# A state-space stage on one core: another order of the side work, and states multiplied in place

## The chip, the cores and the metric

The kernel runs on one core of a Trainium2 chip. The metric is the device time of one execution in microseconds (us), the median of several runs. The engines are named as in the profile: PE is TensorE, DVE is VectorE, ACT is ScalarE, POOL is GpSimd, and SP is the engine whose queue issues most transfers.

## The reference

The input is an image batch x of shape 4 x 96 x 64 x 64. The first of three blocks turns it into four sequences of 4096 positions with 96 channels and runs two state-space layers over them. A layer is, cut to what matters:

```
h     = layernorm(seq)
xs, z = split(h @ in_w)                       # 192 channels each
xc    = silu(causal_conv4(xs) + conv_b)
dt, B, C = split(xc @ xproj_w)                # 6, 16 and 16 columns
delta = softplus(dt @ dt_w + dt_b)
dA    = exp(delta * A)                        # per channel and 16 states
dBx   = delta * B * xc
state[t] = dA[t] * state[t-1] + dBx[t]        # along the 4096 positions
y     = sum_over_states(state * C) + Dp * xc
seq   = seq + (y * silu(z)) @ out_w
```

A fusion with a pooled vector and a batch norm close the block. A convolution block and an attention and feed-forward block in the frequency domain follow; the change doesn't touch them.

## The kernel before

The function `_mamba` holds the state-space stage. The positions are cut into 8 chunks (ch) of 512, the four sequences into two pairs (pr), and there are two layers (l): 32 *units*. The order of units goes by chunk: layer 0 of pair 0, layer 1 of pair 1 of the chunk before, layer 0 of pair 1, layer 1 of pair 0. A unit has 2 x 192 channels x 16 states. They are done in 24 *steps*: k is the channel block (0 to 2), r the group of rows (0 to 3), h the half (0 or 1), so 768 steps in all. Two steps (h = 0 and 1) make a group g, and share one states tile.

A step s of the main loop does the following, and each engine gets its instructions in just this order, written out by hand:

- `broadcasts` (PE, L447) spreads rows of u = delta * xc over the partitions into a PSUM tile pq. u comes as two parts, ux and uy, so that PE's products keep float32's digits. `product` (DVE, L457) multiplies pq by B in place.
- `decays` (ACT, L452) makes dA from delta, which `copies` (SP, L434) fetches, replicated, from DRAM (ddl) into the tile a five steps ahead.
- In four steps of a unit, numbers 2, 6, 10 and 14 (`apart`; called split steps below), the roles differ: u is fetched replicated into db (from ddu), the product with B is POOL's (L457 with db), and the decay goes to pq.
- `scans` (DVE, L470) runs two scans of 512 positions into the states tile hs, starting from hst, the end states of the chunk before. Between the two scans DVE does the product of the next step, except ahead of a split step. Then POOL multiplies the states by C into a tile hc (L476). hs and hc are rings of two.
- `states` (ACT, L480), after every second step, copies the last column of hs to hst.
- `reduce` (PE, L488) sums over the states, three steps after a group began. `gate` (DVE L496, POOL L497) makes y of a channel block after eight steps.

Beside this runs *side work*, in generators that yield between pieces; `Side.slot` emits one piece, and the loop gives one slot to each step (two in the units numbered 0, 1 and 30). There are these lanes. `front(unit)` makes the inputs of the next unit: projections mm_i (L264, L267), silu (L279, L280), mm_dbl (L287, L290) with dbl, dh and dx (L293 to L303), mm_d (L311, L313) with dl (L315), the transfers bc, softplus (L322, emitted in L601), ddl, du = delta * xc on POOL (L339), and the parts ux, uy and ul (L352, L355) with their transfers. `tail(unit)` is the output projection mm_o (L369 to L371) of the unit before, from step 3 on; its result is s (L375), or ft in the second layer (L380). `norm(unit)` is the layer norm of the unit after next, from step 10 on: mm_xc (L203), xc and sq on ACT (L197, L199), mm_v (L214), ve, vh and r on ACT, twelve small Newton steps for the inverse root on POOL (L227 to L230), mm_r (L240), and hn on DVE (L249). `rest` holds batch statistics. At the end of a unit `side.drain()` emits all side work that is left.

Of the kernel before, what the change touches and what calls it, by code (L numbers as in the profile page):

```python
# [48 lines left out]
def _mamba(ctx, tc, io, w, fd, fstats, xsums):  # L49
# [26 lines left out]
    A, HS, HC = ("a", 0, 2, 6), ("hs", 0, 4, 2), ("hc", 0, 4, 2)  # L76
# [12 lines left out]
    out_wT = staged(io["out_wT"], "out_wT", [C, 2, 128], *HC)  # L89
# [12 lines left out]
    dtH = stage("dtH", [128, NL, 256], *HC)  # L102
# [66 lines left out]
    seq, made, ys = {}, {}, {}  # L169
    pqs, das, dbs, hss, hcs, pys = {}, {}, {}, {}, {}, {}  # L170
# [18 lines left out]
    def norm(unit):  # L189

        ch, l, pr = unit
        bs = (2 * pr, 2 * pr + 1)
        xc, sqs, ps = {}, {}, {}

        def centred(n):
            xc[n] = tl(f"xc{n}", unit, [C, TC])
            nc.scalar.copy(xc[n], ps[n])  # L197
            sqs[n] = tl(f"sq{n}", unit, [C, TC])
            nc.scalar.activation(sqs[n], xc[n], AF.Square)  # L199

        for n, b in enumerate(bs):
            ps[n] = mm(f"xc{n}", unit, [C, TC])
            nc.tensor.matmul(ps[n], ctr, seq[b, ch, l], start=True, stop=True)  # L203
            if l == 0:
                nc.scalar.activation(
                    tl("xs", unit, [C, TC], to=f"sq{n}"), seq[b, ch, 0], AF.Identity, accum_out=xsums[:, b, ch : ch + 1]
                )
            yield
            centred(n)
            yield "free" if n == 0 else "gap"  # L210
        p_v = mm("v", unit, [128, 8])
        for n in range(2):
            for j in range(4):
                nc.tensor.matmul(  # L214
                    p_v[:, n * 4 + j : n * 4 + j + 1], sqs[n][:, j * 128 : (j + 1) * 128], mean1, start=True, stop=True
                )
        yield
        ve = tl("ve", unit, [128, 8])
        r = tl("r", unit, [128, 8])
        vh = tl("vh", unit, [128, 8])  # L220
        a = tl("ra", unit, [128, 8])
        nc.scalar.activation(ve, p_v, AF.Identity, bias=w["eps"])
        nc.scalar.activation(vh, ve, AF.Copy, scale=-0.5)
        yield "gap"
        nc.scalar.activation(r.bitcast(I32), ve.bitcast(I32), AF.Identity, bias=magic, scale=-0.5)
        for _ in range(3):
            nc.gpsimd.tensor_tensor(a, r, r, ALU.mult)  # L227
            nc.gpsimd.tensor_tensor(a, a, vh, ALU.mult)
            nc.gpsimd.tensor_scalar(a, a, 1.5, None, ALU.add)
            nc.gpsimd.tensor_tensor(r, r, a, ALU.mult)  # L230
        if ch:
            for b in bs:
                hn = hn_buf[b, l]
                nc.scalar.copy(hn[:, 0:3], hn[:, TC:])
        yield "gap"
        yield "gap"
        for n, b in enumerate(bs):
            p = mm(f"r{n}", unit, [C, TC])
            for j in range(4):
                nc.tensor.matmul(  # L240
                    p[:, j * 128 : (j + 1) * 128],
                    r[:, n * 4 + j : n * 4 + j + 1].to_broadcast([128, C]),
                    ident,
                    start=True,
                    stop=True,
                )
            yield
            yield
            nc.vector.tensor_tensor(hn_buf[b, l][:C, 3:], p, xc[n], ALU.mult)  # L249
            yield "free"  # L250

    def front(unit):

        ch, l, pr = unit
        bs = (2 * pr, 2 * pr + 1)
        for j in range(6):
# [13 lines left out]
            if j == 0:  # L270
                xcv = tl("xcv", unit, [128, 3, TC], bufs=2)
            if j == 3:
                zs = tl("zs", unit, [128, 3, TC], bufs=2)
# [29 lines left out]
        nc.gpsimd.tensor_tensor(dx, dbl, lo, ALU.add)  # L303
        yield "gap"
        dl = tl("dl", unit, [128, 3, TC])
        bcs = []
        for k in range(3):
# [8 lines left out]
            if k == 1:  # L316
                for at in range(2):
                    t = tl(f"bc{at}", unit, [128, 2, TC], bufs=2)
                    src = ddb[at].rearrange("s n t -> s (n t)")[:, None].to_broadcast([DS, 8, 2 * TC])
                    nc.sync.dma_start(t.rearrange("p n t -> p (n t)"), src)  # L320
                    bcs.append(t)
# [6 lines left out]
        us, parts, dus, cut = [], [], [], []  # L328
        made[unit] = [xcv, zs, *bcs, dd, us, parts]
        for at in range(6):  # L330
# [26 lines left out]
            yield "gap"  # L357

    def tail(unit):
# [4 lines left out]
        for n in range(2):  # L364
# [13 lines left out]
            else:  # L378
                ft = work.tile([C, TC], F32, name=f"ft_{tag(unit)}_{n}", tag="ft", bufs=2)
# [6 lines left out]
    def way_out(unit):  # L386
# [11 lines left out]
        for n in range(2):  # L398
            b = 2 * pr + n
            nc.vector.bn_stats(fstats[:, b, ch, :], po[:C, n, :])  # L400
            ft = work.tile([C, TC], F32, name=f"ft_{tag(unit)}_{n}", tag="ft", bufs=2)
# [57 lines left out]
    def scans(s):  # L459
# [15 lines left out]
        sl = slice(2 * h, 2 * h + 2)  # L475
        (nc.gpsimd if s + 1 < n_steps else nc.vector).tensor_tensor(hcs[g][:, sl, :], hss[g][:, sl, :], bc(unit, 3, k, h), ALU.mult)  # L476

    def states(g):
        ch, l, pr = steps[2 * g][0]
        nc.scalar.copy(hst[pr, l, g % 12], hss[g][:, :, TC - 1])  # L480

    def reduce(g):
# [3 lines left out]
        hc = hcs.pop(g)  # L486
# [13 lines left out]
    class Side:  # L500
# [26 lines left out]

        def drain(self):
# [4 lines left out]
    n_steps = len(steps)  # L533
    with tc.manual_schedule():
# [3 lines left out]
        side.drain()  # L538
        for s in range(5):
# [7 lines left out]
        for s in range(n_steps + NS):  # L547
# [33 lines left out]
            if n == 0 or n + 1 in late:  # L581
# [5 lines left out]
            if live and s + 5 < n_steps:  # L587
                unit, k, r, h = steps[s + 5]
                while unit not in made or apart(s + 5) and len(made[unit][5]) <= k:
                    side.slot()  # L590
                copies(s + 5)
# [4 lines left out]
            if at == NS - 1 and n + 1 < len(units):  # L596
                side.drain()
# [956 lines left out]
```

## Time and profile before

| what | value |
|---|---|
| median of 3 runs | 5238.29 us (5235.17 to 5256.56) |
| profiled execution | 5239.08 us |
| its span in the profile | 5237.3 us |
| the state-space stage in it | 93 to 3085 us |
| share of the span busy: PE, DVE, ACT, POOL | 78%, 83%, 51%, 57% |
| mean granted clock of PE | 0.819 |

A row of a waits view gives the engine and instruction that waited, what was taken to release it, the total in us, how often, and the longest. In a timeline a row gives start, duration, engine, line, operation, output and inputs with their shapes, and in brackets the idle time before it with its supposed releaser. The releaser is inferred from semaphore events; where an instruction waits for several, the one named need not be the one that was late. A row of a lines view ends with busy time, mean duration in ns, and the idle time before.

### The profile page before, as it was taken

To read this page: it belongs to the slowest core of one execution; us is meant where nothing else is said; L and a number is where in the kernel's file an instruction comes from. 1 tells how busy PE (TensorE), PEld (TensorE's weight loads), DVE (VectorE), ACT (ScalarE), POOL (GpSimd) and SP (SyncE) were. 2 spreads that over 40 slices of the span, in tenths; PEclk is the share of its full clock that TensorE was granted. 3 is DMA by queue.
4 is the path that set the end of the run, shared out by engine and by line. 5 is a ranking of instruction groups with operands and counts; after the bars stand their busy time and mean duration, and the time that the engine had idled before them with its cause. 6 is when DMAs were issued, how large, how long until landed. Compare 5 with 4: busy or idle time off the path is not lost.

```text
span 5237.3 us, 52687 instructions
## 1 busy us (share of the span) xinstructions
PE 4069.8 (78%) x15440; PEld 1747.5 (33%) x15440; DVE 4322.3 (83%) x5639; ACT 2693.7 (51%) x5149; POOL 2988.1 (57%) x2105
## 2 busy tenths in 40 slices
PE   5677777777777777777777637899898899989776
PEld 2222222222222222222222102345455555545565
DVE  2879899898989989899998887879787978787655
ACT  3565666656566665656656520024453544434566
POOL 2878888888888888888888860002130312212122
PEclk7767877777787777778787658999999999999977
DMA  4768888888887888888788765553325233332110
GB/s 100 179 168 192 197 193 205 195 197 195 197 195 192 209 196 193 195 197 202 186 208 196 175 168 157 165 174 94 95 86 155 85 98 97 100 90 79 53 33 21
DMA packets 314046, 800.19 MB, mean 153 GB/s; under 512 B 52247, under 2 KB 58106, under 8 KB 312702
## 3 DMA queue, kind: packets, MB, share of 16 engines
q1 hardware_dynamic: 310174, 790.53, 59.8%
q10 hardware_dynamic: 3584, 6.29, 0.4%
q8 instruction: 123, 2.02, 0.2%
q14 instruction: 165, 1.35, 0.1%
HBM read 703.83 MB, written 67.63 MB: 147 GB/s over the span
## 4 chain that ended last, share of the span: by engine, by line
PE 26%; DVE 24%; issue 15%; POOL 11%; ACT 9%; DMA 7%; SPq 1%; DVEq 0%; POOLq 0%; ACTq 0%
DVE hs L470 10%; PE py L895 10%; DVE pq L457 6%; DMA a<-ddl 5%; POOL hc L476 4%; PE py L488 2%; DVE z L880 2%; ACT a L452 2%; DVE a L1110 2%; PE px L1177 2%; PE ph L1092 2%; PE pa L1078 2%; PE mm_i L264 2%; POOL t L1248 1%; PE pv L1133 1%
## 5 line engine op out<-in xcount | busy, mean ns | idle before, releaser
L476 POOL TENSOR_TENSOR hc<-hs,bc 128x1024 f32<-128x1024 f32 x767 | 1803.2, 2360 | 318.4 <-DVE hs L470 305.7
L470 DVE TENSOR_TENSOR_SCAN hs<-a,hst,pq 128x512 f32<-128x512 f32 x1280 | 1575.0, 1263 | 40.1 <-ACT hst L480 17.3
L895 PE MATMUL py<-z,wk 128*96 128x512 f32 x2304 | 1113.1, 612 | 25.0 <-issue 14.0
L452 ACT ACTIVATE a<-a,aneg 128x512 f32<-128x512 f32 x1280 | 846.1, 711 | 223.4 <-DMA a<-ddl 216.1
L880 DVE TENSOR_TENSOR z<-cp,cp 128x512 f32<-128x512 f32 x1152 | 794.9, 717 | 183.7 <-PE py L895 169.0
L457 DVE TENSOR_TENSOR pq<-pq,bc 128x1024 f32<-128x1024 f32 x640 | 773.2, 1208 | 111.6 <-PE pq L447 111.5
L488 PE MATMUL py<-hc,red 128*32 128x512 f32 x3072 | 672.3, 840 | 39.4 <-POOL hc L476 39.4
L895 PEld LDWEIGHTS py<-z,wk 128*96 128x96 f32 x2304 | 366.9, 169 | 448.7 <-issue 318.9
L447 PE MATMUL pq<-uy,sel 64*128 64x512 f32 x768 | 262.9, 643 | 281.1 <-DVE hs L470 275.1
L470 DVE TENSOR_TENSOR_SCAN hs<-pq,hst,db 128x512 f32<-128x512 f32 x256 | 325.5, 1271 | 148.1 <-POOL dx L303 95.0
L1145 POOL MEMSET zz<- 96x2 f32 x16 | 1.6, 98 | 738.5 <-ACT zz L1154 738.5
L264 PE MATMUL mm_i<-hn,wk 97*128 97x512 f32 x512 | 297.7, 710 | 118.3 <-ACT xcv L275 93.2
L1246 POOL TENSOR_TENSOR o<-o,fb 128x384 f16<-128x384 f16 x64 | 67.0, 1047 | 547.1 <-ACT o L1251 544.1
L452 ACT ACTIVATE pq<-a,aneg 128x512 f32<-128x512 f32 x256 | 177.0, 692 | 343.5 <-DMA a<-ddl 249.3
L457 POOL TENSOR_TENSOR db<-db,bc 128x1024 f32<-128x1024 f32 x128 | 302.0, 2360 | 23.8 <-DMA db<-ddu 23.8
L447 PEld LDWEIGHTS pq<-uy,sel 64*128 64x128 f32 x768 | 97.9, 234 | 568.4 <-DVE hs L470 431.7
L447 PE MATMUL pq<-ux,sel 64*128 64x512 f32 x512 | 181.5, 635 | 96.4 <-DVE hs L470 76.6
L275 ACT ACTIVATE xcv<-mm_i,pvec 128x512 f32<-128x512 f32 x96 | 66.0, 687 | 313.1 <-PE mm_i L264 147.8
L1177 PE MATMUL px<-bd,a 128*96 128x128 f32 x1024 | 148.2, 293 | 67.1 <-DVE a L1110 56.2
L1146 POOL TENSOR_TENSOR zz<-zz 96x256 f32<-96x256 f32 x128 | 122.8, 959 | 133.4 <-ACT zz L1153 81.3
L264 PEld LDWEIGHTS mm_i<-hn,wk 97*128 97x128 f32 x512 | 98.7, 214 | 291.1 <-issue 165.5
L447 PEld LDWEIGHTS pq<-ux,sel 64*128 64x128 f32 x512 | 66.9, 231 | 305.3 <-DVE hs L470 212.0
(286 smaller groups left out, 6534.3 us busy)
## 6 DMA issues: line engine op xcount, KB each, us to landing
a<-ddl SPq DMA_DIRECT2D x768, 512.0 KB, 6.8
cp<-p SPq DMA_DIRECT2D x480, 192.0 KB, 2.7
db<-ddu SPq DMA_DIRECT2D x128, 512.0 KB, 9.0
bc<-ddb SPq DMA_DIRECT2D x64, 512.0 KB, 7.8
cp<-p SPq DMA_DIRECT2D x480, 64.0 KB, 2.7
ddl<-dl SPq DMA_DIRECT2D x128, 192.0 KB, 3.9
tw_k_fwd<-in_k_fwd SPq DMA_DIRECT2D x64, 256.0 KB, 3.4
tw_k_inv<-in_k_inv SPq DMA_DIRECT2D x64, 256.0 KB, 3.1
```

Source lines behind the costliest of these rows:

```text
L264: nc.tensor.matmul(p, wt[:, 0:128], hn_buf[bs[k], l][:, cols], **f)
L447: nc.tensor.matmul(pqs[s][:, i, :], sel[rows, r, :], made[unit][6][k][h][rows], start=True, stop=True)
L452: nc.scalar.activation(to[:, i, :], das[s][:, i, :], AF.Exp, scale=acol(s, i))
L457: engine.tensor_tensor(t, t, bc(unit, 2, k, h), ALU.mult)
L470: nc.vector.tensor_tensor_scan(hss[g][:, at, :], d0[:, i, :], d1[:, i, :], hst[pr, l, g % 12][:, at : at + 1], ALU.mult, ALU.add)
L476: (nc.gpsimd if s + 1 < n_steps else nc.vector).tensor_tensor(hcs[g][:, sl, :], hss[g][:, sl, :], bc(unit, 3, k, h), ALU.mult)
L488: nc.tensor.matmul(pys[unit, k][32 * (i // 2 + i % 2 * 2) :][:32], red[:, r, :], hc[:, i, :], start=(r == 0), stop=(r == 3))
L880: nc.vector.tensor_tensor(zs[n], cps[q, r0], cps[q, r1], ALU.mult)
L895: nc.tensor.matmul(pys[q], wk[k // KG][:, k % KG, :], zs.pop(n), start=(k == 0), stop=(k == NE - 1))
L1078: nc.tensor.matmul(pa[j][:, jj, :], kf[:, 2 * (j % 2) + jj, :], dd[j][:, jj, :], start=True, stop=True)
L1146: nc.gpsimd.tensor_tensor(z0[:, :, 0, :], z0[:, :, 0, :], z1[:, :, 0, :], ALU.add)
L1177: nc.tensor.matmul(p[:, j, :], a2[i % 2][:, kk, :], tabs["bd"][:, int(kk > 0), :], start=True, stop=True)
```

## The change

What it does, in the order of the diff:

- The side work has another order. `front` of a unit may begin a whole unit earlier: at step 4 of unit n, norm and front of unit n+2 are queued together (the latter in a lane of its own, `ahead`, that becomes the front lane at the next unit's start), and front waits until its norm is done. The loop gives a second slot in every odd step, so 36 a unit for 24, and the drain at a unit's end is gone.
- `front` ends with du; the fetches bc and ddu and the parts ux, uy and ul move into a generator `split`, in a lane that comes first, and are made one channel block at a time (steps 5, 13 and 21 of the unit before its own).
- dx on POOL is not issued where it is made but kept in `side.post` and issued behind the next product with C.
- Copies may stay behind and catch up (`copied`), where they had to be five steps ahead.
- States are multiplied by C in place, in hs, without the last column; hs becomes a ring of three and hc is gone. ACT multiplies the last column, after the copy to hst, with one or two small instructions per group.
- xcv and zs are rings of three, and ft uses the buffers of sq.

```diff
             nc.vector.tensor_tensor(hn_buf[b, l][:C, 3:], p, xc[n], ALU.mult)
+            if n == 1:
+                normed.add(unit)
             yield "free"
 
     def front(unit):
 
         ch, l, pr = unit
         bs = (2 * pr, 2 * pr + 1)
+        while unit not in normed:
+            yield "gap"
...
-                xcv = tl("xcv", unit, [128, 3, TC], bufs=2)
+                xcv = tl("xcv", unit, [128, 3, TC], bufs=3)
...
-                zs = tl("zs", unit, [128, 3, TC], bufs=2)
+                zs = tl("zs", unit, [128, 3, TC], bufs=3)
...
         dx = tl("dx", unit, [128, TC], F32R)
-        nc.gpsimd.tensor_tensor(dx, dbl, lo, ALU.add)
+        side.post.append(lambda: nc.gpsimd.tensor_tensor(dx, dbl, lo, ALU.add))
         yield "gap"
         dl = tl("dl", unit, [128, 3, TC])
-        bcs = []
         for k in range(3):
...
-            if k == 1:
-                for at in range(2):
-                    t = tl(f"bc{at}", unit, [128, 2, TC], bufs=2)
-                    src = ddb[at].rearrange("s n t -> s (n t)")[:, None].to_broadcast([DS, 8, 2 * TC])
-                    nc.sync.dma_start(t.rearrange("p n t -> p (n t)"), src)
-                    bcs.append(t)
         _softplus(nc, work, dl)
         yield "gap"
 
         dd = dp.tile([2, 32, 3, 2, TC], F32, name=f"ddl_{tag(unit)}", tag="ddl")
         for q in range(4):
             nc.sync.dma_start(dd[q % 2, :, :, q // 2, :], dl[32 * q : 32 * q + 32])
-        us, parts, dus, cut = [], [], [], []
-        made[unit] = [xcv, zs, *bcs, dd, us, parts]
-        for at in range(6):
+        us, parts, dus = [], [], []
+        made[unit] = [xcv, zs, None, None, dd, us, parts]
+        while side.low:
+            yield "gap"
+        for ks in ((0, 1), (2,)):
+            for k in ks:
+                dus.append(tl(f"du{k}", unit, [128, TC], to="du", bufs=3))
+                nc.gpsimd.tensor_tensor(dus[k], dl[:, k, :], xcv[:, k, :], ALU.mult)
+            if len(ks) == 2:
+                yield "gap"
+        side.low.append(split(unit, ddb, dus, us, parts))
+
+    def split(unit, ddb, dus, us, parts):
+
+
+        cut, start = [], NS * units.index(unit) - NS
+        while side.step < start + 2:
+            yield "gap"
+        for at in range(2):
+            t = made[unit][2 + at] = tl(f"bc{at}", unit, [128, 2, TC], bufs=2)
+            src = ddb[at].rearrange("s n t -> s (n t)")[:, None].to_broadcast([DS, 8, 2 * TC])
+            nc.sync.dma_start(t.rearrange("p n t -> p (n t)"), src)
+        yield "gap"
+        for at in range(1, 6):
+            if at > 1:
+                yield "gap"
             if at == 2:
                 for k in range(2):
                     ddu = dp.tile([32, 2, TC], F32, name=f"ddu{k}_{tag(unit)}", tag=f"ddu{k}")
                     for i in (0, 1):
                         nc.sync.dma_start(ddu[:, i, :], dus[k][64 * i : 64 * i + 32])
                     us.append(ddu)
-            for k in ((0, 1), (2,))[at] if at < 2 else ():
-                dus.append(tl(f"du{k}", unit, [128, TC], to="du", bufs=3))
-                nc.gpsimd.tensor_tensor(dus[k], dl[:, k, :], xcv[:, k, :], ALU.mult)
             if at >= 3:
 
                 x, y, t = (t.bitcast(F32) for t in cut[at - 3])
...
-            while at == 3 and side.step < NS * units.index(unit) - 3:
+            while at < 4 and side.step < start + 8 * at - 3:
                 yield "gap"
-            if 1 <= at < 4:
+            if at < 4:
...
-            yield "gap"
...
-                ft = work.tile([C, TC], F32, name=f"ft_{tag(unit)}_{n}", tag="ft", bufs=2)
+                ft = work.tile([C, TC], F32, name=f"ft_{tag(unit)}_{n}", tag=f"sq{n}", bufs=1)
...
-            hss[g] = scan.tile([128, 4, TC], F32, name=f"hs_{name(s)}", tag="hs")
-            hcs[g] = scan.tile([128, 4, TC], F32, name=f"hc_{name(s)}", tag="hc")
+            hss[g] = scan.tile([128, 4, TC], F32, name=f"hs_{name(s)}", tag="hs", bufs=3)
...
-        sl = slice(2 * h, 2 * h + 2)
-        (nc.gpsimd if s + 1 < n_steps else nc.vector).tensor_tensor(hcs[g][:, sl, :], hss[g][:, sl, :], bc(unit, 3, k, h), ALU.mult)
+        sl, LC = slice(2 * h, 2 * h + 2), TC - 1
+        (nc.gpsimd if s + 1 < n_steps else nc.vector).tensor_tensor(hss[g][:, sl, :LC], hss[g][:, sl, :LC], bc(unit, 3, k, h)[:, :, :LC], ALU.mult)
 
     def states(g):
-        ch, l, pr = steps[2 * g][0]
-        nc.scalar.copy(hst[pr, l, g % 12], hss[g][:, :, TC - 1])
+
+        unit, k, r, h = steps[2 * g]
+        ch, l, pr = unit
+        end = hss[g][:, :, TC - 1]
+        nc.scalar.copy(hst[pr, l, g % 12], end)
+        col_c = made[unit][3][:, :, TC - 1 : TC]
+        for i in (k,) if k < 2 else (0, 1):
+            e = end if k < 2 else end.rearrange("p (h i) -> p i h", i=2)[:, i]
+            nc.scalar.activation(e, e, AF.Copy, scale=col_c[:, i])
 
     def reduce(g):
         unit, k, r, h = steps[2 * g]
         if r == 0:
             pys[unit, k] = ps_y.tile([128, TC], F32, name=f"py_{name(2 * g)}", tag="py")
-        hc = hcs.pop(g)
+        hc = hss.pop(g)
...
-            self.front, self.tail, self.norm, self.rest, self.held, self.step = [], [], [], [], None, 0
+            self.low, self.tail, self.front, self.norm, self.ahead, self.rest, self.held, self.step = [], [], [], [], [], [], None, 0
+            self.post = []
+
+        def flush(self):
+
+            while self.post:
+                self.post.pop(0)()
 
         def slot(self):
+            self.flush()
             waiting = []
             while True:
                 lane = self.held
                 if lane is None:
-                    lanes = (self.front, self.tail, [] if self.tail else self.norm, self.rest)
+                    lanes = (self.low, self.tail, self.rest, self.front, [] if self.tail else self.norm, self.ahead)
...
+        def turn(self):
+
+            if self.held is self.ahead:
+                self.held = self.front
+            self.front += self.ahead
+            self.ahead.clear()
+
...
+    copied = [5]
...
-                if n + 1 < len(units) and n + 1 not in late:
-                    side.front += ([norm(units[n + 1])] if n == 0 else []) + [front(units[n + 1])]
-                    side.norm += [weights(1)] * (n == 0)
+                side.turn()
+                if n == 0:
+                    side.front += [norm(units[1]), front(units[1])]
...
-                if at == 8:
+                if at == 2:
                     load(units[n + 2])
-                if at == 10:
+                if at == 4:
                     (side.front if n + 1 in late else side.norm).append(norm(units[n + 2]))
+                    side.ahead.append(front(units[n + 2]))
...
-            if n == 0 or n + 1 in late:
+            if n == 0 or n + 1 in late or s % 2 == 1:
...
+            side.flush()
+            while live and copied[0] < min(s + 6, n_steps):
+                unit, k, r, h = steps[copied[0]]
+                while unit not in made or apart(copied[0]) and len(made[unit][5]) <= k:
+                    if copied[0] > s + 5:
+                        break
                     side.slot()
-                copies(s + 5)
+                else:
+                    copies(copied[0])
+                    copied[0] += 1
+                    continue
+                break
             if s % 2 == 0 and 0 < s <= n_steps:
                 states(s // 2 - 1)
             if s % 8 == 2 and 2 < s <= n_steps + 2:
                 gate(s // 2 - 2)
-            if at == NS - 1 and n + 1 < len(units):
-                side.drain()
+                side.flush()
 
```

More of the change, by code (lines that the diff above doesn't have):

```diff
@@ L74, in stage @@
         return t.rearrange("p (a m) -> p a m", a=shape[1]) if len(shape) == 3 else t
-    A, HS, HC = ("a", 0, 2, 6), ("hs", 0, 4, 2), ("hc", 0, 4, 2)
+    A, HS = ("a", 0, 2, 6), ("hs", 0, 4, 3)
     def staged(src, name, *where):
@@ L88, in _mamba @@
     fus_w = _load(nc, wp, io["fus_wT"][0:C, :], [C, C], "fus_w")
-    out_wT = staged(io["out_wT"], "out_wT", [C, 2, 128], *HC)
+    out_wT = staged(io["out_wT"], "out_wT", [C, 2, 128], *HS)
     selF = staged(io["k_sel"].rearrange("c (j m) -> c j m", j=4), "selF", [128, 4, 128], *A)
@@ L100, in _mamba @@
     nc.vector.tensor_copy(sel, selF)
-    dtH = stage("dtH", [128, NL, 256], *HC)
+    dtH = stage("dtH", [128, NL, 256], *HS)
     nc.vector.tensor_copy(dtH.bitcast(F32R), dtF)
@@ L167, in _mamba @@
     NS = 24
-    seq, made, ys = {}, {}, {}
-    pqs, das, dbs, hss, hcs, pys = {}, {}, {}, {}, {}, {}
+    seq, made, ys, normed = {}, {}, {}, set()
+    pqs, das, dbs, hss, pys = {}, {}, {}, {}, {}
     def tag(unit):
@@ L400, in way_out @@
             nc.vector.bn_stats(fstats[:, b, ch, :], po[:C, n, :])
-            ft = work.tile([C, TC], F32, name=f"ft_{tag(unit)}_{n}", tag="ft", bufs=2)
+            ft = work.tile([C, TC], F32, name=f"ft_{tag(unit)}_{n}", tag=f"sq{n}", bufs=1)
             nc.scalar.copy(ft, po[:C, n, :])
@@ L553, in _mamba @@
             if at == 0:
-                if n + 1 < len(units) and n + 1 not in late:
-                    side.front += ([norm(units[n + 1])] if n == 0 else []) + [front(units[n + 1])]
-                    side.norm += [weights(1)] * (n == 0)
+                side.turn()
+                if n == 0:
+                    side.front += [norm(units[1]), front(units[1])]
+                    side.norm += [weights(1)]
             if at == 22 and n + 1 == len(units):
@@ L586, in _mamba @@
                 scans(s)
-            if live and s + 5 < n_steps:
-                unit, k, r, h = steps[s + 5]
-                while unit not in made or apart(s + 5) and len(made[unit][5]) <= k:
-                    side.slot()
-                copies(s + 5)
+            side.flush()
[4 more added lines that the diff above has]
+                        break
+                    side.slot()
+                else:
[3 more added lines that the diff above has]
+                break
             if s % 2 == 0 and 0 < s <= n_steps:
@@ L595, in _mamba @@
                 gate(s // 2 - 2)
-            if at == NS - 1 and n + 1 < len(units):
-                side.drain()
+                side.flush()
 def _softplus(nc, pool, t):
```

## The prediction

> **What bounds the kernel now.** I read the page first, then busy time in three windows (ahead of the state-space stage, the stage, what follows).
>
> ```profile
> core 0: us, PE busy (x) PEld busy (x) DVE busy (x) ACT busy (x) POOL busy (x), PEclk, DMA share, GB/s
> 93.00:3085.00 2992.00, 2208.75 (x7423) 684.36 (x7425) 2667.20 (x2366) 1782.57 (x3090) 2549.77 (x1579) 0.75 0.81 192
> 3085.00:5237.00 2152.00, 1819.08 (x7922) 1045.92 (x7916) 1648.51 (x3263) 884.28 (x2019) 419.59 (x434) 0.92 0.34 101
> ```
>
> The diff touches only the middle 2992 us. VectorE (DVE) is busy in 2667.2 of them, so 325 us is all that the change can remove without less DVE work, and it keeps DVE's work. GpSimd (POOL) follows with 2549.8, at an unchanged amount of work (511 of 512 columns are still its own). So the question is DVE's idle time: its waits in the stage.
>
> ```profile
> DVE hs L470 <- POOL dx L303: 95.0, 28, 4.0
> DVE hn L249 <- PE mm_r L240: 71.9, 35, 11.1
> DVE pq L457 <- PE pq L447: 63.0, 40, 3.2
> DVE hs L470 <- POOL hc L476: 35.6, 30, 3.8
> DVE hs L470 <- ACT hst L480: 27.5, 9, 5.4
> DVE hs L470 <- issue: 21.1, 20, 4.9
> ```
>
> The first label misleads, since no scan reads dx. The timeline of one such wait:
>
> ```profile
> 1102.62 1.23 DVE L457 TENSOR_TENSOR pq<-pq,bc 128x1024 f32<-128x1024 f32 x1 [1.88 <-PE pq L447]
> 1107.10 0.58 ACT L293 COPY dbl<-mm_dbl 128x512 f32<-128x512 f32 x1 [3.32 <-PE mm_dbl L290]
> 1109.17 1.28 POOL L303 TENSOR_TENSOR dx<-dbl,dh 128x512 fp32r<-128x512 f32 x1 [1.61 <-ACT dh L297]
> 1110.22 0.18 ACT L480 COPY hst<-hs 128x4 f32<-128x4 f32 x1
> 1110.49 1.28 DVE L470 TENSOR_TENSOR_SCAN hs<-pq,hst,db 128x512 f32<-128x512 f32 x1 [3.11 <-POOL dx L303]
> ```
>
> The scan starts 0.09 us after the copy of end states ends (1110.40). That copy reads the states buffer that the scan, two groups later, overwrites: a ring of two. ScalarE (ACT) comes to it late because it stood 3.32 us for a projection on TensorE (PE) ahead of it. The copy's releases explain 8.75 us of each pair of units (1.15 + 3.95 + 0.54 + 3.11), late broadcasts 4.2 (0.72 + 1.60 + 1.88), mm_r 3.7, POOL 0.84: 17.5 of the 184.4 us of a steady pair. A steady unit is thus 92.2 us, 83.5 without its stalls, or 3.48 us a step. A step ahead of a split step has no DVE product and takes 2.4.
>
> **The change, part by part.** *Ring of three in place.* A scan now waits for the reduction three groups back, two steps later than before. Gone: 4.4 us per steady unit, and about 52 us in the first three and last two units, where the same wait is dense. What is late next is not the buffer but the two chains below. The in-place product over 511 columns goes at 2.36 us as before (the row of L476); the other bound is 0.5 us more each if the shorter rows cost time, 767 of them, partly under POOL's waits.
>
> *End column on ACT.* 512 small ACT instructions, nearest rows 0.18 us (hst, 128x4) and 0.27 us (ve, 128x8): 16 a unit, 3 to 4 us of an engine busy 1783 of 2992 us. Their price is not that time but their place: the reduction on PE now waits for an instruction at the end of ACT's step, behind side work that itself waits for PE. Behind the reduction stand PE's side matmuls and the next broadcasts, and DVE waits for those. Today the reduction waits for POOL alone. Bounds: nothing, to 7 us a unit (the long silu block, 1.28 + 1.48 + 1.47, and mm_dbl ahead of it, as in the 3.32 us wait above). I take 4, near the late broadcasts of today (2.1) and the stands of ACT (3.3).
>
> *First moved chain: step 2 to step 10.* Norm and output projection now follow each other at once, and the Newton steps of the inverse root on POOL stand ahead of the product of step 7 and of db for split step 10, which scan 10 reads. Before, they stood in step 18, with no db behind them. Counted from the end of step 2's db:
>
> ```profile
> L476 POOL TENSOR_TENSOR hc<-hs,bc 128x1024 f32<-128x1024 f32 x604 | 1420.3, 2359 | 242.3 <-DVE hs L470 239.9
> L497 POOL TENSOR_TENSOR y<-y,zs 128x512 f32<-128x512 f32 x76 | 96.6, 1271 | 0.0
> L214 PE MATMUL mm_v<-mean,sq 96*128 96x1 f32 x416 | 92.9, 353 | 0.0
> L601 ACT ACTIVATE dl<-dl 128x1536 f32<-128x1536 f32 x26 | 38.6, 1485 | 0.3
> L601 ACT ACT_TABLE_LOAD x26 | 33.4, 1283 | 0.5
> ```
>
> POOL: du2 1.27, three products 7.08, y2 1.27, at 9.6. PE: two mm_o, each 4.0 (the lines view of PE has 40.5, 34.2 and 29.5 us busy at L371, L370 and L369 for 26 of them), at 17.6; s 0.57; mm_xc 1.1; xc and sq 1.2; ux and uy with the second xc and sq 2.4; mm_v 92.9/26 = 3.57, at 26.5. ACT: ve, vh, r 0.8 and a decay pair 1.33, at 28.6. POOL: twelve small ones 3.4 (1042.37 to 1045.75 in the timeline), product 2.36, db 2.36, at 36.7. DVE's own eight steps with y and hn take 27. Stall 9.7 at these means. Less: a full clock makes PE's 12.7 us shorter by 2.6 (a broadcast takes 0.50 then, 0.63 in the mean), and ux, uy and the decay pair may fall elsewhere, 2.6: stall 4.5. It can't go below nothing. I take 6.5, between; it holds what is left of today's mm_r waits (1.9).
>
> *Second chain: step 20 to the next unit's step 2.* dx comes behind product 20, softplus ends in step 23, and du0, du1 stand ahead of product 23 and the next db. After scan 20: product and dx 3.7; mm_d 0.6, dl 0.7; decay pair, dl, decay pair 3.3; end states 0.7; dl 0.7; table 1.28 and softplus 1.49; du0, du1 2.5; product 2.36; db 2.36: 19.7. DVE's five steps take 16.3. Stall 3.4; 0.7 if the decays fall elsewhere, 5 if mm_d waits for a reduction ahead of it (1.7). I take 3.5.
>
> *At nothing*: SP's earlier DMAs (bc a unit ahead; the burst of twelve in step 23 stands ahead of decay copies that have five steps' lead, with 6.8 us from issue to landing); ft in the squares' buffers (bn_stats frees it at once). If that cover is gone, one copy of 6.8 us a unit.
>
> *The sum.* A steady unit: 83.5 + 4 + 6.5 + 3.5 = 97.5, for 92.2: +5.3. With 27 steady units, +143. The five edge units: 52 us of copy waits and 13 of a norm done inline go, about 8 each of chain stalls comes: -25. The profiled execution (span 5237.3, 1.8 around it, 5239.1 in all, 0.8 over the median of 5238.3) becomes 5357; against the median 5356.
>
> A rule on the clock bears on the first chain. The row first: while PE was busy in all of a window, its clock stood at half.
>
> ```profile
> 1096.20:1100.80 4.60, 3.51 (x6) 0.88 (x6) 4.55 (x4) 2.36 (x5) 4.14 (x3) 0.78 0.67 151
> 1100.80:1105.40 4.60, 4.60 (x16) 0.78 (x14) 2.78 (x3) 1.86 (x3) 3.72 (x3) 0.50 0.42 114
> 1105.40:1110.00 4.60, 3.92 (x20) 0.78 (x16) 1.98 (x2) 2.83 (x5) 2.99 (x2) 0.98 0.16 36
> ```
>
> The Trainium skill, "TensorE: Matmul & The Clock Gate", Part 1, says that the gate is at half rate by default and that about 3.4 us of activity opens it to full. By that rule a denser run of PE work, as the change makes in steps 3 to 9, would be slow for its first 3.4 us only, and the first chain's stall would be an estimated 8.8 with all else at its mean, about 25 us off the total. The trace only half agrees: the clock did rise after that window, but it had fallen during work, and over the stage the mean is 0.75. I keep the means.
>
> **Rivals.** *The chains arrive in time, faster.* POOL waits 305.7 us for scans in the stage, about 10 us a unit. If y2, softplus and the root reach POOL inside those waits, and PE holds a full clock through steps 3 to 9, both db are ready. It decides where the first chain is under 30 us rather than 36.7 and the second under 17. DVE and POOL alone, each in its queue order, then set about 86.3 a unit: -5.9 x 27 = -159, -40 at the edges, 5040; with 1 to 4 us of stalls left, 5060 to 5150. Against it: du0 and du1 stand ahead of product 23 whatever the clock. *They cancel, no change*: 9 us of stalls replace 8.75: 5213 to 5265. *PE becomes the bound*: it has 69 us of work a unit, and with each reduction tied to ACT every stand of one engine passes to the other; a late reduction then also holds the states buffer, so the ring doesn't do what it says. With 7 for the lockstep, 9.7 and 5 it is 105 a unit: 5560.
>
> **How the numbers follow.** The forecast, slower between 5265 and 5480, 0.45; PE as the bound, above 5480, 0.16; no change 0.09; faster 0.30. Half a per cent, 26 us, is about what a measurement of this kernel tells from none. The range leaves out a tenth on each side: 5115 to 5540. Faster 0.30, same 0.09, slower 0.61; the likeliest case's own range is 5265 to 5480.
>
> **What would show it.** Right: no scan waits any more with an hst copy just ended; instead the scans of split steps 10 and 2 wait for POOL's db, with the root's small instructions or du0 and du1 ahead of it, 3 us and more each, once a unit, and DVE is busy in the same 2667 us of a longer stage. PE's reduction waits for ACT where it waited for POOL. Wrong: those waits under 1 us, a period under 90 us, DVE's share above 93%. The clock tells which side of the sum failed: well over 0.80 in the stage, the PE terms were too long.

## The result, and the profile after

The changed kernel takes 5690.02 us (median of 4 runs, 5680.98 to 5696.39), the kernel before 5243.43 in the same sessions: ratio 1.0848, interval 1.0819 to 1.0877. That is 447 us slower. The direction was forecast, but the time lies above the range. The profiled execution has a span of 5689.1 us.

The windows row of the stage, with the columns shown for before:

```profile
93.00:3535.00 3442.00, 2263.04 (x7429) 692.71 (x7429) 2677.54 (x2370) 1920.08 (x3604) 2545.70 (x1579) 0.70 0.69 168
```

The stage grew from 2992 to 3442 us, the part behind it stayed (2154 us). DVE is busy for the same 2.7 ms; its idle time went from 325 to 764 us, and the clock from 0.75 to 0.70. Counted from the first scan of one unit to that of the next, units 6 to 28 take 105.7 us each (from 792.9 to 3223.0) where they took 92.1. DVE's waits in the stage (engine and instruction, what released it, total us, times, longest):

```profile
DVE pq L473 <- PE pq L463: 318.3, 121, 9.4
DVE hn L249 <- PE mm_r L240: 146.7, 29, 9.2
DVE hs L485 <- POOL db L473: 124.8, 39, 5.1
DVE fstats L424 <- ACT ft L396: 72.5, 29, 5.9
DVE hs L485 <- ACT a L468: 49.8, 32, 8.9
```

The scans' waits behind the hst copy are gone. In their place stand late broadcasts, five times what they were, hn, the db of the split steps, and a wait that before had no row: batch statistics behind ft. PE's own waits say why broadcasts are late:

```profile
PE py L510 <- ACT hs L502: 598.9, 214, 8.6
PE pq L463 <- DVE hs L485: 325.3, 177, 4.9
```

The reduction stands for the last column from ACT for 599 us. The longest such stand of one unit, first in ACT's timeline, then in PE's:

```profile
1825.40 1.28 ACT L283 ACT_TABLE_LOAD   x1
1826.70 1.49 ACT L283 ACTIVATE xcv<-xcv 128x1536 f32<-128x1536 f32 x1
1828.09 1.47 ACT L284 ACTIVATE zs<-zs 128x1536 f32<-128x1536 f32 x1
1829.57 1.28 ACT L468 ACT_TABLE_LOAD   x1
1830.87 2.56 ACT L468 ACTIVATE a<-a,aneg 128x512 f32<-128x512 f32 x4
1833.33 0.18 ACT L498 COPY hst<-hs 128x4 f32<-128x4 f32 x1
1833.60 0.48 ACT L502 ACTIVATE hs<-hs,bc 128x2 f32<-128x2 f32 x2
```

```profile
1834.00 2.07 PE L510 MATMUL py<-hs,red 128*32 128x512 f32 x8 [7.84 <-ACT hs L502]
1836.00 1.74 PE L291 MATMUL mm_dbl<-xcv,xp 128*64 128x512 f32 x4
1838.67 0.50 PE L463 MATMUL pq<-ux,sel 64*128 64x512 f32 x2
```

0.48 us of work holds PE for 7.84 us, since silu, two table loads and four decays are queued ahead of it; the broadcast behind the reduction starts 4.7 us later still. What reaches DVE of it is the wait for that broadcast:

```profile
1839.22 1.23 DVE L473 TENSOR_TENSOR pq<-pq,bc 128x1024 f32<-128x1024 f32 x1 [2.79 <-PE pq L463]
```

The second chain looks as drawn in the prediction. POOL's timeline, then DVE's:

```profile
1745.00 2.50 POOL L332 TENSOR_TENSOR du<-dl,xcv 128x512 f32<-128x512 f32 x2 [5.03 <-DMA ux<-ul]
1747.45 2.35 POOL L491 TENSOR_TENSOR hs<-hs,bc 128x1022 f32<-128x1022 f32 x1
1749.76 2.35 POOL L473 TENSOR_TENSOR db<-db,bc 128x1024 f32<-128x1024 f32 x1
```

```profile
1752.14 1.28 DVE L485 TENSOR_TENSOR_SCAN hs<-pq,hst,db 128x512 f32<-128x512 f32 x1 [4.40 <-POOL db L473]
```

The scan of step 2 waits 4.40 us. The 5.03 us on POOL are for softplus, which du reads and which ended 0.08 us before it; the transfer named there is none that du reads.

### The profile page after: what moved, and what is told of

Read it like the earlier page. It is cut to its first block, busy times and chain, and to the rows that moved or that the text cites. A ratio compares the mean times of both kernels' runs of the same rounds, so it can differ in the third digit from the quotient of the medians.

```text
span 5689.1 us, 53738 instructions
## 1 busy us (share of the span) xinstructions
PE 4122.4 (72%) x15440; PEld 1754.4 (31%) x15440; DVE 4330.7 (76%) x5639; ACT 2830.8 (50%) x5661; POOL 2980.9 (52%) x2105
## 5 line engine op out<-in xcount | busy, mean ns | idle before, releaser
L491 POOL TENSOR_TENSOR hs<-hs,bc 128x1022 f32<-128x1022 f32 x767 | 1798.7, 2357 | 418.9 <-DVE hs L485 412.4
L510 PE MATMUL py<-hs,red 128*32 128x512 f32 x3072 | 726.2, 919 | 677.0 <-ACT hs L502 598.9
L463 PE MATMUL pq<-uy,sel 64*128 64x512 f32 x768 | 241.0, 622 | 320.3 <-DVE hs L485 320.1
L510 PEld LDWEIGHTS py<-hs,red 128*32 128x32 f32 x3072 | 104.6, 128 | 883.9 <-issue 386.1
L332 POOL TENSOR_TENSOR du<-dl,xcv 128x512 f32<-128x512 f32 x96 | 120.4, 1269 | 159.2 <-ACT dl L647 144.0
L268 PEld LDWEIGHTS mm_i<-hn,wk 97*128 97x128 f32 x512 | 114.5, 237 | 196.7 <-issue 135.1
```

The costliest lines, as they stand in the source:

```text
L268: nc.tensor.matmul(p, wt[:, 0:128], hn_buf[bs[k], l][:, cols], **f)
L463: nc.tensor.matmul(pqs[s][:, i, :], sel[rows, r, :], made[unit][6][k][h][rows], start=True, stop=True)
L510: nc.tensor.matmul(pys[unit, k][32 * (i // 2 + i % 2 * 2) :][:32], red[:, r, :], hc[:, i, :], start=(r == 0), stop=(r == 3))
```

## The experiments

Two theories at first. L: the loss comes from the link that the last column makes from ACT to PE's reduction. C: it comes from the order of the side work, the link being a symptom. "Changed" below is the changed kernel, "before" the one before. Ratios are to runs of before on the same chip.

**e2, the states in place, side work as before.** `scans`, `states`, `reduce` and the ring of three from the changed kernel in the kernel before.

> The kernel before with its side work as it was, and only the states in place: a ring of three, 511 columns on POOL, the last column on ACT. Theory L: the third buffer takes away the waits behind the hst copy (up to 170 us), but the reduction's wait for ACT costs more: 5300 to 5450. Theory C: the ring's gain is there alone, about 5240 - 170 = 5070 to 5120.

5306.41 us, ratio 1.0122 (1.009 to 1.0154), at the low end of theory L's range. The edit by itself already loses, though 65 us and not 447. DVE's broadcast waits in the stage are 255.5 us for 63.0, and PE waits for ACT's last column 221.7 us.

**e5, the same without ACT.** Cut to the operands that change:

```diff
-hss[g][:, at, :]   (scan)          +hss[g][:, at, 1:]      # tile of TC + 1 columns
-hss[g][:, sl, :LC] * C[:LC]        +hss[g][:, sl, :TC] = hss[g][:, sl, 1:] * C
-nc.scalar.activation(e, e, AF.Copy, scale=col_c[:, i])
```

> The kernel before with its own side work, and states in place in a ring of three without any work for ACT: the scan writes columns 1 to 512 of a tile of 513, the product with C goes to columns 0 to 511, and column 512 keeps the end state for the copy to hst. So the third buffer alone, with no link from ACT to the reduction. Theory L: e2's late broadcasts (304 us of waits) fall back to those of before (63), the waits behind the hst copy stay away: 5240 - 120 to 170, about 5090. Rival (the third buffer only moves each wait to the broadcast behind it, link or not): 5210 to 5310.

5177.78 us, ratio 0.9874 (0.9855 to 0.9892): faster than before, 128 us under e2. The third buffer is worth 66 us, not 170:

```profile
DVE pq L457 <- PE pq L447: 155.7, 120, 4.5
DVE hn L249 <- PE mm_r L240: 67.6, 45, 3.3
```

No scan waits for a copy any more, but broadcast waits rose from 63.0 to 155.7: more than half of the gain went to the next late thing, as the rival said, though not all of it. In units 6 to 28 a unit takes 90.1 us, for 93.1 in e2 and 92.1 before.

**e6, the changed kernel without ACT's last column.** The edit of e5 in the changed kernel.

> The changed kernel with the same shifted product, so no last column on ACT and no link from ACT to the reduction. Theory L: PE's 599 us of waits for the last column go, with them most of DVE's 318 us for broadcasts and the 50 for decays: about 5690 - 300 = 5390. Theory C (the moved chains set the time): the broadcasts are late because of mm_o, norm and projections themselves: 5640 or more.

5375.61 us, ratio 1.0259 (1.0233 to 1.0285): 314 us back, as L said. DVE's waits in the stage, broadcasts and db:

```profile
DVE pq L473 <- PE pq L463: 141.1, 80, 9.4
DVE hs L485 <- POOL db L473: 72.8, 29, 4.5
```

The link costs 128 us in the old order and 314 in the new, 4.0 and 9.8 for each of the 32 units. What is left, 198 us over e5, is the rest of the change: the order of the side work, with ft's buffers. In units 6 to 28 a unit takes 95.6 us: 10.1 less than in the changed kernel, 5.4 more than in e5.

**e17, a control.** In e5 and e6 POOL's product also became shorter (2.18 us for 2.36). Cut to the operands that change:

```diff
-hcs[g][:, sl, :] = hss[g][:, sl, :] * C      # hs of TC columns
+hcs[g][:, sl, :] = hss[g][:, sl, 1:] * C     # hs of TC + 1, rings of two kept
```

> The kernel before, its rings of two (hs and hc) kept, only that the scan writes columns 1 to 512 of a tile of 513, so that POOL's product reads from column 1 and writes to hc. In e5 and e6 POOL's product took 2.18 us and not 2.36: this run tells whether that comes from the shift, and what it is worth by itself. If POOL's 0.18 us per step is on the path: 5200 to 5220, and a part of what e5 and e6 gained is not the link's. If POOL's waits for scans (306 us) cover it: 5230 to 5245.

5244.83 us, ratio 1.0003 (0.9992 to 1.0014), with POOL's product at 2.18 us: in the kernel before that is worth nothing by itself. In the changed kernel's order no run has the shorter product with the link kept, so a part of e6's 314 us, in the waits for db above all, could be POOL's.

**e11, the same link at another place in ACT's queue.** `states(s // 2 - 1)` stands before `side.slot()`, not at the step's end.

> The changed kernel with the copy to hst and the last column issued at the beginning of ACT's even step, ahead of that step's side work and decays, and not at its end. Same instructions, same link. If the link costs by its place in ACT's queue: well under the 314 us of the link stay, 5450 to 5550. If it costs by being there at all: 5690, or more, since decays now stand behind the scans.

5568.44 us, ratio 1.0626 (1.0606 to 1.0647). The same instructions and the same link, 122 us less, and PE's waits for the last column fall from 599 to 301 us: a good third of the link's price was its place behind one step's side work. POOL's product is the changed kernel's here, so this part doesn't rest on e6's shorter one. Earlier steps' side work still stands ahead of it.

**e4 and e9, ft in buffers of its own.** `tag=f"sq{n}"` becomes `tag=f"s{b}"`: in e4 in the changed kernel, in e9 in e6.

> The changed kernel, with ft in the buffers of s (read for the last time by the same unit's mm_o) and not in those of sq, so that xs on ACT waits neither for the transfer fd nor for the batch statistics. Theory L: ACT's stand of 3.6 us in each second unit goes, and the broadcast wait of 3.4 us behind it: 16 x 3.4 = 54 us, about 5635. Theory C: what is saved is lost at hn: 5690.

> The changed kernel with the shifted product (no link from ACT to the reduction) and ft in the buffers of s. What is left is the order of the side work. If ft's price (80 us in e4) was paid through the link, as ACT's stand reached PE by way of the last column, without the link it costs less: 5340 to 5376. If it is paid at hn and the batch statistics too: 5295.

e4: 5609.63 us, ratio 1.0695 (1.0659 to 1.0731), 80 us less. e9: 5336.69, ratio 1.0183 (1.0167 to 1.02), 39 less than e6. What shared the buffer, in ACT's timeline of the changed kernel:

```profile
1768.62 0.31 ACTq L397 DMA_DIRECT2D fd<-ft  x1
1772.54 0.63 ACT L205 ACTIVATE xs<-x 96x512 f32<-96x512 f32 x1 [3.95 <-DMA fd<-ft]
```

xs must wait until ft has left for DRAM. ACT stands 3.95 us, and through the link PE after it; half of the price goes with the link.

What is left in e9, DVE's waits in the stage:

```profile
DVE hn L249 <- PE mm_r L240: 124.5, 28, 10.6
DVE pq L473 <- PE pq L463: 110.3, 58, 7.3
DVE hs L485 <- POOL db L473: 72.5, 29, 4.3
DVE fstats L424 <- ACT ft L396: 49.4, 27, 3.1
DVE hs L485 <- ACT a L468: 32.6, 33, 8.0
```

Against e5: hn +57, broadcasts -45, db +63 (9.4 in e5), statistics +49, decays +33 (e5 has no such row): 157 of the 159 us between the two kernels. The next runs try to take these waits away one by one.

**e7 and e8, du behind the db.**

```diff
-        while side.low:
+        while side.low or side.step < NS * units.index(unit) - NS + 1:
-                nc.gpsimd.tensor_tensor(dus[k], dl[:, k, :], xcv[:, k, :], ALU.mult)
+                side.post.append(lambda k=k: nc.gpsimd.tensor_tensor(dus[k], dl[:, k, :], xcv[:, k, :], ALU.mult))
```

e7 has this in the changed kernel; e8 has it in e9, with one more `yield` ahead of hn.

> The changed kernel with du0, du1 and du2 issued a step later, behind the db product of the next unit's first split step, so that this db no longer stands behind softplus. Theory C: the scans' waits for db go (125 us) and what follows comes earlier: 5690 - 125 = 5565, or less. Theory L: the time that db gave PE to catch up is lost at the broadcasts and at hn: 5640 to 5690.

> The changed kernel with four things undone or moved: shifted product (no link), ft in the buffers of s, du behind db, and hn one slot further behind mm_r. If the four losses add up (300 + 80 + 125 + about 100 of hn's 147): about 5085, below the kernel before. If they hide one another: 5250 to 5400.

e7: 5719.23 us, ratio 1.0914 (1.0889 to 1.0939), slower than the changed kernel. e8: 5501.04, ratio 1.049 (1.0468 to 1.0512), slower than e9. DVE's waits in the stage of e7:

```profile
DVE pq L473 <- PE pq L463: 322.3, 126, 9.4
DVE fstats L424 <- ACT ft L396: 146.8, 29, 6.5
DVE hn L249 <- PE mm_r L240: 140.5, 29, 8.9
```

The waits for db are gone, as meant (7.9 us are left), and the statistics' wait has doubled. DVE waits for ft, and ft for mm_o. It isn't y2 on POOL, behind du, that holds mm_o: in a dozen steady units of the trace y2 is ready before mm_o begins. mm_o stands on PE behind a reduction that has waited 4.0 to 5.3 us, and in seven of the twelve its two results then take 12.5 us, each pair of matmuls 2.02, where they took 8.0 in the changed kernel.

e8 lies above both of its forecasts. hn's wait is gone (9.2 us left), but the waits for db grew to 117.3, and those for broadcasts and ft to 254.0 and 131.7.

**e10, the output projection and all behind it two steps later** (in e9: `at == 3` becomes 5, `at == 4` becomes 6, outside the edge units).

> As e9, but the output projection and what follows it (norm, then front) begin two steps later, at step 5 for 3. mm_o then no longer stands on PE for the y2 that POOL has just been given, the root's twelve small instructions come behind the db of step 10, and du0 and du1 behind the db of the next unit's step 2. Theory C (in the order of the side work both chains into a db, and mm_o behind y2, are the cost): the waits for db (69 us in e6) and most of those for hn (130), broadcasts (131) and statistics (47) go: 5376 - 200 = 5130 to 5180, near e5. Rival (the side work as such is too dense on PE): 5300 or more.

5578.54 us, ratio 1.0644 (1.0619 to 1.067), 242 us slower than e9. Theory C fails in this form. DVE's waits in the stage:

```profile
DVE pq L473 <- PE pq L463: 217.6, 95, 9.4
DVE fstats L424 <- ACT ft L396: 141.2, 29, 5.9
DVE hs L485 <- POOL db L473: 133.9, 54, 4.8
```

Only hn's wait fell (124.5 to 90.0). PE's timeline in one unit shows the statistics' part: each mm_o takes 6 us, each pair of its matmuls 2.02 us, where the means of before gave 4.0 us for all three pairs.

```profile
1723.29 2.02 PE L385 MATMUL mm_o<-y,of_w 128*96 128x512 f32 x2 [2.28 <-ACT ft L396]
1725.24 2.02 PE L386 MATMUL mm_o<-y,of_w 64*96 64x512 f32 x2
1727.19 2.02 PE L387 MATMUL mm_o<-s,fus_w 96*96 96x512 f32 x2
```

That is a matter of the clock (0.50 while these matmuls ran), and common to the runs that lost. In units 6 to 28 the same 276 matmuls of mm_o keep PE busy for 150 us in e9, at a mean clock of 0.75, but for 251 in e10 (0.69), 241 in e8 (0.70) and 229 in e7 (0.69; 169 and 0.72 in the changed kernel). A slow mm_o need not cost anything: it is 190 us in e5, where DVE has no wait for ft. Whether the low clock causes the losses of e7, e8 and e10 or follows from PE's stands, no run separates.

**e13 and e16, small side results issued further behind their makers.** e13: four more `yield "gap"` ahead of the statistics, in e9. e16: that, and one more `yield` ahead of hn.

> As e9, with the batch statistics on DVE issued some three steps later, when ft has long been written; nothing else moves. If DVE's waits for ft (49 us) are a price of their own: 5337 - 49 = 5288. If DVE would only come earlier to a broadcast that is late anyway: 5325 to 5345.

> As e13, and hn issued one slot further behind mm_r, which moves front and du one step later too. If DVE's waits for small side results are what is left of the order's cost: 5288 - 80 = 5210. If the lateness passes on to db and the broadcasts, as in e8 and e10: 5350 to 5500.

e13: 5324.41 us, ratio 1.0154 (1.0135 to 1.0173): the statistics' 49 us of waits vanish, 12 us of time come back (the intervals of e9 and e13 overlap a little). e16: 5479.4, ratio 1.0462 (1.0429 to 1.0496). Its waits in the stage:

```profile
DVE pq L476 <- PE pq L466: 290.9, 138, 10.2
DVE hs L488 <- POOL db L476: 108.9, 59, 6.1
DVE hs L488 <- ACT pq L471: 87.0, 23, 4.9
DVE hs L488 <- ACT a L471: 50.2, 40, 9.1
DVE hn L250 <- PE mm_r L240: 12.5, 7, 3.0
```

hn's wait is nearly gone; broadcasts, db and decays take more than its place, and mm_o keeps PE busy for 225 us, nearly as in e8 and e10. So the 159 us of e9 over e5 are not five prices: but for e13, whichever result was given room, the lateness moved on and grew.

**e14, e15 and e18, more matmuls for a higher clock.** In `broadcasts`, `for _ in range(2):` (in e18 3) around the matmul; e14 in the changed kernel, e15 and e18 in e5.

> The changed kernel with each broadcast matmul issued twice (the second writes the same values), 1280 more matmuls of 0.5 to 0.64 us on PE, to see whether a busier PE is given a higher clock (0.70 in the changed kernel's stage). Theory K (the low clock is a cause of the loss): the clock goes to 0.85 and more, mm_o, norm and projections shorten by a fifth, 5500 to 5600. Theory L (PE is slow because it stands waiting for ACT; the clock follows): more work on the engine that is late, 5750 to 5900.

> The same doubling in e5, the fastest so far, where no link to ACT holds PE. Theory K: a clock over 0.85 in the stage, late broadcasts (156 us) halved, 5100 to 5150. If PE's added 0.5 to 1 us per step outweighs it: 5200 to 5300.

> As e15 with each broadcast matmul issued three times. If the clock goes on rising (0.75, 0.81, then over 0.85 in the stage) and PE keeps its slack: 5130 to 5150. If the added work now shows at the broadcasts that DVE waits for: 5160 to 5200.

e14: 5706.08 us, ratio 1.0881 (1.0863 to 1.09), with a clock of 0.74 in the stage for 0.70. Neither forecast came: the clock rose less than theory K (the low clock as a cause) needs, and the loss is smaller than L's. In e6, with the same side work and no link, the clock is 0.73 too. So here it seems to follow PE's stands; that is argued, not shown. e15: 5151.66, ratio 0.9819 (0.9802 to 0.9837). e18: 5152.65, ratio 0.9836 (0.9804 to 0.9868). The windows rows of e15 and e18:

```profile
93.00:2980.00 2887.00, 2238.89 (x8685) 739.25 (x8685) 2662.91 (x2364) 1782.63 (x3088) 2413.33 (x1578) 0.81 0.84 199
93.00:2980.00 2887.00, 2276.09 (x9939) 822.84 (x9939) 2654.84 (x2356) 1787.94 (x3089) 2409.93 (x1576) 0.86 0.84 200
```

1280 more matmuls cost PE hardly any busy time (2216.3 us in the stage of e5, clock 0.75), since all of them run faster, and save 26 us of the total, though the broadcast waits hardly fell (155.7 to 143.7; half was forecast); 1280 more save nothing further. e15 is faster than both kernels, by 1.8% against before.

**e1, e3 and e12, the last column on DVE.** e1 in the changed kernel, e3 in e2:

```diff
-nc.scalar.copy(hst[pr, l, g % 12], end)
+nc.vector.tensor_copy(hst[pr, l, g % 12], end)
-nc.scalar.activation(e, e, AF.Copy, scale=col_c[:, i])
+nc.vector.tensor_scalar(e, e, col_c[:, i], None, ALU.mult)
```

e12 is e3 with `tensor_tensor(..., end, end, ALU.max)` and a `tensor_tensor` with C in their place.

> The changed kernel, with the copy to hst and the product of the last column on DVE, so that the reduction no longer waits for ACT. Theory L (the link from ACT to the reduction makes most of the loss): PE's waits for the last column (599 us) go, and with them most of DVE's waits for broadcasts (318 us in the stage); some 900 tiny DVE instructions cost 60 to 100 us: about 5690 - 320 + 90 = 5460, lower still if hn and the batch statistics come earlier too. Theory C (the moved chains set the time, the link is a symptom): the broadcasts stay late, 5700 or more. In both, the scans' waits for db (125 us) stay.

> As the kernel before with the states in place in a ring of three, but the copy to hst and the last column on DVE. Both theories: no scan waits for a copy by ACT; up to 170 us less for the ring, 60 to 100 more for the tiny DVE instructions: 5140 to 5180. A rival (the ring only moves the wait to the next late thing): 5300 or more.

> As e3 (before's order, copy to hst and last column on DVE), but as two-input instructions (maximum of the column with itself, product with C) for the copy and the product with a scalar. In e3 these took 0.49 and 0.99 to 1.52 us in the mean, 0.14 and 0.23 where POOL was idle: they seem to wait until POOL's product is through. If that belongs to the kind of instruction, 768 of them now cost 0.15 each, 115 us: 5178 + 115 = 5290. If any DVE instruction that small waits for POOL: 5800 as in e3.

e1: 5877.57 us, ratio 1.1224 (1.1155 to 1.1294). e3: 5807.22, ratio 1.1073 (1.1045 to 1.1102). e12: 5605.74, ratio 1.0705 (1.0668 to 1.0743). As tests of the link they say little, since the tiny instructions cost far more than expected; in e1 DVE's broadcast waits did fall, from 318 to 71 us. Two timelines of e12, DVE and POOL:

```profile
1498.55 2.27 DVE L488 TENSOR_TENSOR hs<-hs,bc 128x4 f32<-128x4 f32 x1
1506.74 0.17 DVE L485 TENSOR_TENSOR hs<-hs,bc 128x4 f32<-128x4 f32 x1
```

```profile
1498.45 2.34 POOL L475 TENSOR_TENSOR hs<-hs,bc 128x1022 f32<-128x1022 f32 x1
1506.82 2.35 POOL L475 TENSOR_TENSOR hs<-hs,bc 128x1022 f32<-128x1022 f32 x1 [1.23 <-DVE hst L482]
```

An instruction of one form takes 0.17 us when POOL is idle as it starts, and 2.27 when it starts 0.10 us behind POOL's product; it then ends 0.03 us behind it.

## Why the prediction was wrong

The forecast built a steady unit as 83.5 us without stalls, 4 for the link and 10 for the two chains: 97.5. Units 6 to 28 measure 90.1 (e5: the ring without the link, old order), 10.1 more for the link (changed kernel over e6) and 5.4 for the rest of the change (e6 over e5): 105.7. So two terms were too small, and one too large.

*The link: mis-sized.* The prediction named it, with its place as the price, and took 4 us a unit from bounds of 0 to 7. Over all 32 units it is 4.0 in the old order (128 us) and 9.8 in the new (314). The upper bound was one stand of ACT; in a steady unit of the changed kernel PE stands 3.3, 0.8, 4.9, 7.8 and 4.5 us for the last column, 21 us. The missing 5.8 us a unit are 186 us.

*The unit without stalls: too small.* 4.4 us a unit and 52 at the edges, some 170 us, were taken off for the ring; without the link it is 66 in the old order (e5; in the new order no run measures it). Starting from 83.5 also took off today's late broadcasts, 2.1 a unit, for which no reason was given. "What is late next is not the buffer but the two chains" named the wrong successor: in e5, where the chains are as before, broadcasts are late next, 155.7 us or 4.9 a unit.

*At nothing: ft in the squares' buffers.* The prediction looked at the statistics that free the buffer and not at the transfer to DRAM that reads it too. 80 us in the changed kernel (e4), 39 without the link; both are parts of the prices above, and these errors can't be added up.

*The edges: wrong sign.* -25 us was forecast for the first three and last two units. By their first scans they take 67 us more than before, and 21 more without the link (e6), so most of it goes with the link. The two slots per step in units 0, 1 and 30 can't explain it, since the kernel before has them too; what makes the 21 us is open.

*The two chains: right in size, wrong in use.* 6.5 and 3.5 us were taken. The second measured 4.4 us, at scan 2, as drawn. The first measured 5.1 (146.7 us over 29), but at hn, which stands ahead of scan 10 in DVE's queue, and not at the db. Yet no run got these microseconds back: e7, e8 and e16 took one of these waits away, e10 a part of one, and they lost 29 to 242 us against the kernel that they altered. The prediction added stalls as if each were a price, 10 us a unit where the rest of the change costs 5.4. What it costs as a whole is shown (198 us without the link, 39 of them ft); which part of it costs the rest stays open.

*The rival "PE becomes the bound"*, given 0.16, had the unit right: 105 us, measured 105.7. In part that is luck: it takes 83.5, 7 for the lockstep, 9.7 and 5, where 90.1, 10.1 and 5.4 were measured. PE is busy in 2263 of the stage's 3442 us, so it is PE's stands that bind and not its work. Its total, 5560, fell short mostly by the edges. Its clause that a late reduction would also hold the states buffer did not come true: no scan waits for the reduction.

*The clock.* The stage's clock fell to 0.70. Three windows of the changed kernel; in the first PE did nothing:

```profile
1770.40:1774.80 4.40, 0.00 (x0) 0.00 (x0) 4.40 (x5) 2.17 (x6) 2.35 (x1) 0.74 1.03 316
1774.80:1779.20 4.40, 4.18 (x12) 0.88 (x12) 1.52 (x2) 3.18 (x8) 2.35 (x1) 0.50 1.03 244
1779.20:1783.60 4.40, 4.40 (x20) 3.78 (x18) 3.58 (x3) 4.17 (x10) 0.00 (x0) 0.50 0.32 76
```

In the other two PE is busy for 8.6 of 8.8 us, all at half clock (0.50). The Trainium skill ("TensorE: Matmul & The Clock Gate", Part 1) would have opened the gate after about 3.4 us of activity; here 8.6 us of it were not enough, so the prediction did well not to take 25 us off by that rule. That denser work raises the clock, as the page says, e15 and e18 show.

## What to carry to other kernels

An instruction's price is its place: before a small operation is given to another engine, look at what that engine's queue holds ahead of it and at what stands behind the instruction that will wait for it; here at most 0.5 us of ACT work at a time held PE for up to 8.6 us. Where a value has to survive an in-place operation, a tile one column wider and a shifted write keeps it without a third engine. Stalls read off a trace don't add up to a gain: give one result more room, and the next one in the queues may be later by more. Ask also what clock PE then has: in the runs that lost, the same projection kept PE busy for a third to two thirds longer.

## What the runs showed of the hardware

DVE instructions of 2 to 4 elements per partition, reading and writing SBUF alone (e1, e3, e12), took a mean of 0.5 to 1.5 us; in timelines of e3 and e12 they took 0.13 to 0.23 us where POOL was idle. The Trainium skill, "SBUF — State Buffer", "Who interferes with whom", tells of ports that DVE and POOL share, under an exclusive lock: a DVE instruction with two SBUF inputs contends with a POOL instruction that reads SBUF, and so does one in a two-port mode. e12's pair of timelines agrees: the DVE instruction that came second ended only behind POOL's. The kernel's products on DVE, which have one input in PSUM, took 1.21 us in the mean in e3 and e12, as before.

POOL's product of 1024 elements took 2.18 us with its input one column off (e5, e6, e17) and 2.36 without (1022 elements in place, 1024 not); the reason stays open.
